# Two image layers on one core: the last band's filter taps held back until the third band of the next image, a reordered start of the query pass, and one band fewer on the array at the end

## The chip, the cores and the metric

The kernel runs on one core of a Trainium2 chip. The metric is the device time of one execution in microseconds (us). The profiler adds, for one execution, when each engine ran which instruction. The engines are named as in the profile: PE is TensorE (matmuls), PEld its weight loads, DVE VectorE, ACT ScalarE, POOL GpSimd, SP SyncE, which issues most of the DMAs.

## The reference

Eight images of 384 channels and 64 x 64 pixels pass through two layers, all in float32. Both add to their input.

```python
x = x + layer0(gn(x))     # gn: group norm over 32 groups
x = x + layer1(gn(x))

# layer 0: linear attention, 6 heads of 64
q = elu(rope(conv1x1(x, Wq)) * scale) + 1
k = elu(rope(conv1x1(x, Wk))) + 1
v = conv1x1(x, Wv)
kv, k_sum = sum_n k v, sum_n k
out = (q @ kv) / (q . k_sum + 1e-6);  conv1x1(out, Wfc)

# layer 1: a 1x1 convolution, a filter in the 8x8 Fourier domain, 3x3 taps, a gate
t = conv1x1(x, w_in);  t = irfft2(rfft2(blocks(t)) * fft_filter)
t = depthwise3x3(t, w_dw)
x1, x2 = t[:, :192], t[:, 192:]
return conv1x1(gelu(x1) * x2, w_out)
```

## The kernel before

An image is cut into eight bands of eight rows (512 pixels). A band is a tile of 128 partitions by three channel tiles by 512 pixels. The loop over images `b` has two passes over the bands of one image.

The first is `queries(b, ...)`: the end of layer 0. For each band, `q_project` makes three `pq` tiles (nine matmuls), the rotation and the elu turn them into `qc` on DVE and ACT (lines 610 to 626, then 337 to 339), `q_normalise` makes the normaliser with matmuls against `ks_bd` (`pn`, line 635) and a short chain of DVE and ACT steps that ends in `parts`, `q_spread` spreads that over the channels (`prb`, line 659) and multiplies `qc` by it (line 668), and `project_out` gives `pf` (line 676), which is added to `x`. Before the first band's output, `keys.finish` turns the accumulated keys and values into a matrix `mt` through `kx`, `ks_bd` and `pm`. Bands run two apart: `pq` of band j + 2, `pn` of band j + 1, `prb` of band j, `pf` of band j - 1.

The second pass is layer 1 of the image, mixed with the keys and values of image b + 1. Per band: `normalised` makes `hf`, `expand_filter` the matmuls `pi` and `pd` and the product `tf`, `back_transform` the matmuls `pb` and the ACT copies into one of two `ring` tiles with a halo row above and below. The last halo row of a band is filled from the band after it. Then `first_taps` (ACT, the first of nine taps), `taps` (24 DVE instructions, eight for each channel tile, line 788), `gate_taps` (gelu on ACT, product on DVE, into the single tile `gated`), and `contraction` (`pw`, lines 815 and 826, four ACT copies into `y`, and a DMA on POOL's queue that adds `y` to the output; line 845). `taps` run one band behind and `contract` two bands behind. The work that is left at the end of an image is done in the next image's `queries`: `before_last` contracts band 6, `gate` does taps and gate of band 7 after the first band's `q_spread`, and `output` contracts band 7 at the third band:

```python
            if j == 0:
                gate()
            ...
            if j == 2 and b < nb - 1:
                output()
            if j in (4, 5):
                load_x(b + 1, j - 4)
```

Between its layer 1 steps, a band of the second pass takes items from `fill`: `pk` and `pv` of a band and the accumulation of keys and values (line 470), 24 small matmuls of 1.6 us per band. Band 0 and band 1 accumulate themselves, band 2 nothing, and later bands the one before:

```python
                fill = chain_of(keys.project(j), keys.accumulate(j - 1 if j > 2 else NBAND))
```

The last image has no next image, so its second pass is a loop of its own. There, in the bands for which `on_array` is true (3, 6 and 7), the third channel tile's nine taps are matmuls with diagonal weights (`array_taps`, `ptap`, line 764), and DVE has 16 taps instead of 24.

The kernel gives the instructions in a written order, and a scheduler then orders each engine's queue by what can run when; for the order on an engine, the built order is shown where it matters. Tiles come from pools: nine `w` tiles, ten `x` tiles (which `y` shares), two `dw` tiles, and eight PSUM banks (`ps_tile`).

Of the kernel before, what the change touches and what calls it, by code (L numbers as in the profile page):

```python
# [9 lines left out]
F32 = mybir.dt.float32  # L10
BF16 = mybir.dt.bfloat16
AF = mybir.ActivationFunctionType
ALU = mybir.AluOpType

P = 128
C = 384
CT = 3
H = W = 64
N = H * W
NBAND = 8  # L20
# [97 lines left out]
def conv_blocks_kernel(ctx: ExitStack, tc: tile.TileContext, a: dict, out: bass.AP, nb: int):  # L118
    nc = tc.nc
# [9 lines left out]
    def ps_tile(name):  # L129
        return psum.tile([P, 512], F32, tag="ps", name=name)  # L130
# [9 lines left out]
    def load_x(b, j):  # L140
        if b >= nb:
            return
        t = xp.tile([P, CT, BT], F32, tag="x", name=f"x_{b}_{j}")
        nc.sync.dma_start(t, x_in[b][:, :, j * BT : (j + 1) * BT])
        xt[b, j] = t
# [96 lines left out]
    ident = groups[:, 2 * CT * NG :]  # L242
# [387 lines left out]
    def q_normalise(b, j, q):  # L630

        pn = ps_tile(f"pn_{b}_{j}")
        for t in range(CT):
            for s in range(4):
                nc.tensor.matmul(
                    pn[32 * s : 32 * s + 32, :P],
                    ks_bd[:, t, :],
                    q[:, t, s * P : (s + 1) * P],
                    start=(t == 0),
                    stop=(t == CT - 1),  # L640
                )
        rn = small.tile([P, P], F32, tag="rn", name=f"rn_{b}_{j}")
        nc.vector.tensor_scalar_add(rn, pn[:, :P], 1e-6)
        nc.vector.reciprocal(rn, rn)

        part = small.tile([P, P], BF16, tag="part", name=f"part_{b}_{j}")
        parts = small.tile([P, P], BF16, tag="parts", name=f"parts_{b}_{j}")
        nc.scalar.copy(part, rn)
        nc.vector.scalar_tensor_tensor(rn, part, take_off[:, 0:1], rn, ALU.mult, ALU.add)
        nc.scalar.copy(part, rn)  # L650
        nc.vector.scalar_tensor_tensor(parts, part, take_off[:, 1:2], rn, ALU.mult, ALU.add)
        return parts
# [19 lines left out]
    def project_out(b, j, q, mt):  # L672
        for m in range(CT):
            p_ = ps_tile(f"pf_{b}_{j}_{m}")
            for t in range(CT):
                nc.tensor.matmul(  # L676
                    p_, mt[:, t, m * P : (m + 1) * P], q[:, t, :], start=(t == 0), stop=(t == CT - 1)
                )
            xm = xt[b, j][:, m, :]
            nc.vector.scalar_tensor_tensor(xm, p_, bfc[:, m : m + 1], xm, ALU.add, ALU.add)  # L680
            if m == 0:
                yield
        if j == 1:
            differences[b] = taps_pool.tile([P, CT, BT], F32, tag="dw", name=f"differences_{b}")
        band_sums(b, 1, j, xt[b, j], differences.get(b))
# [64 lines left out]

    def on_array(b, j):

        return b == nb - 1 and j in (3, NBAND - 2, NBAND - 1)

    def make_diagonals():
        t = small.tile([P, CT, C], F32, tag="wk", name="diagonals", bufs=1).rearrange("p t c -> p (t c)")
# [21 lines left out]
            dw_pe[b, j] = ps_tile(f"ptap_{b}_{j}")  # L778
            array_taps(b, j, range(9 if j == NBAND - 1 else 6))

    def taps(b, j):

        t, acc = ring[j % 2], dw[b, j]
        for m in range(CT - on_array(b, j)):
            for k in range(1, 9):
                src = t[:, m, k // 3 : k // 3 + 8, k % 3 : k % 3 + W]
                wd = w_dw[:, m, k : k + 1]
                nc.vector.scalar_tensor_tensor(acc[:, m], src, wd, acc[:, m], ALU.mult, ALU.add)  # L788

    def gate_taps(b, j):  # L790
        g = gated
# [9 lines left out]
    def depthwise_gate(b, j):  # L801
        taps(b, j)
        gate_taps(b, j)
# [43 lines left out]
    def contract(b, j):  # L847
        run(contraction(b, j))
# [14 lines left out]
    def chain_of(*chains):  # L863
        for c in chains:
            yield from c

    def run(*chains):

        chains = list(chains)
        while chains:  # L870
            chains = [c for c in chains if next(c, chains) is not chains]
# [62 lines left out]
                    sum_weight(self.wv, "wv")  # L934
                self.vbias = v_bias(self.b, self.params)

    def queries(b, keys, before_last, gate, output):


        wq, qbias = keys.wq, keys.qbias  # L940
        q, done = {}, []
        run(q_project(b, 0, wq, qbias, q))
        before_last()
        run(keys.accumulate(NBAND - 1))
        finish = keys.finish(done)
        for _ in zip(q_project(b, 1, wq, qbias, q), finish):
            pass
        prepared = []
        chain = layer0_chain(b + 1, prepared)
        normaliser = {0: q_normalise(b, 0, q[0])}  # L950
        for j in range(NBAND):

            if j < NBAND - 2:
                project = q_project(b, j + 2, wq, qbias, q)
                for _ in range(2 if j else CT):
                    next(project)
                if j == 0:
                    run(finish)
                    mt = done[0]
                if j != 1:  # L960
                    normaliser[j + 1] = q_normalise(b, j + 1, q[j + 1])
                run(project)
            if 2 <= j < NBAND - 2:
                next(chain, None)
            q_spread(b, j, q[j], normaliser.pop(j))
            if j == 0:
                gate()
            if j >= 1:
                output_ = project_out(b, j - 1, q.pop(j - 1), mt)
                if j in (1, NBAND - 2):  # L970
                    next(output_)
                    normaliser[j + 1] = q_normalise(b, j + 1, q[j + 1])
                run(output_)
                if j < NBAND - 2:
                    next(chain, None)
            if j == 2 and b < nb - 1:
                output()
            if j in (4, 5):
                load_x(b + 1, j - 4)
            if j == NBAND - 2:  # L980
                run(chain)
        run(project_out(b, NBAND - 1, q.pop(NBAND - 1), mt))
        return prepared

# [6 lines left out]
    prepared = []  # L991
# [51 lines left out]
    def nothing():  # L1043
        pass

    before_last = gate = output = nothing
    for b in range(nb):
        prepared = queries(b, keys, before_last, gate, output)
        keys = Keys(b + 1, prepared)
        params = []  # L1050
        chain, more = norm_chain(b, 1, params), chain_of(keys.project_k(0), keys.load_values(), keys.project_k(1))
        last = b == nb - 1
        if last:

            more = contraction(b - 1, NBAND - 1) if b else iter(())
        for steps in (2, 0, 1, 1) if last else (2, 1, 1, 3):
            next(chain)
            for _ in range(steps):
                next(more, None)
        run(chain)  # L1060
        ahead = normalised(b, 0, params, (8, 8), "f")
        run(more)
        if last:
            break
        first_values = keys.project_v(0)
        next(first_values, None)
        for j in range(NBAND):
            if j < 2:
                fill = chain_of(keys.project_v(j) if j else first_values, keys.accumulate(j))
            else:  # L1070
                fill = chain_of(keys.project(j), keys.accumulate(j - 1 if j > 2 else NBAND))
            tf = []
            h = normalised(b, j, params, (8, 8), "f") if j else ahead
            store_x(b, j)
            if 1 <= j < NBAND - 1:
                load_x(b + 1, j + 1)
            layer1 = expand_filter(b, j, h, tf)
            items = 1 if j < 2 else 2

            def some(n):  # L1080
                for _ in range(n):
                    next(fill)

            next(layer1)
            some(items)
            run(layer1)
            some(2 * items)
            back_transform(b, j, tf[0])
            first_taps(b, j)
            some(items)  # L1090
            if j > 1:
                contract(b, j - 2)
            run(fill)
            keys.prepare(j)
            if j > 0:
                depthwise_gate(b, j - 1)
            stream_stats(b + 2, j)
        keys.prepare(NBAND)

        def before_last(b=b):  # L1100
            contract(b, NBAND - 2)

        def gate(b=b):
            depthwise_gate(b, NBAND - 1)

        def output(b=b):
            contract(b, NBAND - 1)


    make_diagonals()  # L1110
# [2 lines left out]
    for j in range(NBAND):  # L1113
        tf = []
        layer1 = expand_filter(b, j, h, tf)
        run(layer1)
        store_x(b, j)
        if j < NBAND - 1:
            h = normalised(b, j + 1, params, (8, 8), "f")
        back_transform(b, j, tf[0])  # L1120
        if j and on_array(b, j - 1):

            array_taps(b, j - 1, range(6, 9))
        first_taps(b, j)
        if j >= 2:
            contract(b, j - 2)
        if j >= 1:
            taps(b, j - 1)
            gate_taps(b, j - 1)
# [45 lines left out]
```

## Time and profile before

| | |
|---|---|
| median of three executions | 3442.15 us (3442.06 to 3443.75) |
| profiled execution | 3442.33 us, span 3440.6 us |
| mean granted TensorE clock | 0.989 |
| PE busy | 96% of the span |
| DVE busy | 81% |
| ACT busy | 57% |
| POOL busy | 4% |
| DMA | 336.01 MB, mean 98 GB/s |

The span runs from the first to the last instruction of the profiled execution; 1.7 us lie around it. In a row for a stretch of time stand its bounds and length, then the busy time of PE, PEld, DVE, ACT and POOL, each with its number of instructions, the granted clock, the DMA share and the rate. In a row of a timeline stand the start, the time taken, the engine, the line of the kernel, the operation, output and inputs, and in brackets the idle time before it and what ended it. A float32 matmul leaves two records. The second image's first pass begins at about 570 us and its layer 1 at about 750; each later image lies some 420 us further on, and the last pass runs from about 3240 us to the end.

### The profile page before, as it was taken

The numbers are of one execution on the slowest core, as the hardware profiler recorded it, in microseconds if no ns is written. First come the engines' busy times: TensorE is split into PE (matmuls) and PEld (weight loads), VectorE is DVE, ScalarE is ACT, GpSimd is POOL, SyncE is SP. The second block draws the span as 40 slices with busy tenths as digits, with TensorE's granted clock in tenths as the row PEclk, the third lists the DMA queues.
The fourth block names the chain that finished last, engine by engine and source line by source line (L and its number), as shares of the span: only waits on it lengthen the run. The fifth ranks groups of instructions, "written<-read, shape, count | busy, mean of one in ns | idle before, by whom it ended". The sixth has DMA issues, their size and how long they took to land.

```text
span 3440.6 us, 53200 instructions
## 1 busy us (share of the span) xinstructions
PE 3319.7 (96%) x21374; PEld 1856.2 (54%) x21374; DVE 2786.9 (81%) x4430; ACT 1976.0 (57%) x3854; POOL 143.2 (4%) x247
## 2 busy tenths in 40 slices
PE   8999999999999999999999999989999899999987
PEld 5544565456654566445664456644566445664454
DVE  6587789868898688986889868897788977899597
ACT  4445666556664566555665556655576555555553
POOL 0000001000010000100001000010000000000000
PEclk9999999999999999999999999999999999999999
DMA  6323244332343333442343423334243331333112
GB/s 221 112 89 115 65 111 100 114 124 66 92 112 115 110 84 87 100 131 96 82 108 90 133 90 92 94 98 131 81 111 92 107 121 55 66 83 101 51 27 48
DMA packets 149484, 336.01 MB, mean 98 GB/s; under 512 B 27141, under 2 KB 38389, under 8 KB 141045
## 3 DMA queue, kind: packets, MB, share of 16 engines
q1 hardware_dynamic: 123844, 282.85, 24.5%
q0 software_dynamic: 25200, 49.55, 10.0%
q8 instruction: 168, 2.75, 0.3%
q14 instruction: 80, 0.65, 0.1%
q10 hardware_dynamic: 192, 0.21, 0.0%
HBM read 232.70 MB, written 99.88 MB: 97 GB/s over the span
## 4 chain that ended last, share of the span: by engine, by line
PE 76%; DVE 18%; ACT 4%; issue 1%; DMA 0%; SPq 0%; DVEq 0%; ACTq 0%
PE pi L694 14%; PE pk L438 13%; PE pf L676 13%; PE pv L454 12%; PE pq L597 7%; DVE dw L788 6%; PE pw L815 4%; PE pd L708 2%; PE pb L729 2%; PE pw L826 2%; PE acc L483 2%; PE acc L470 2%; DVE qc L339 1%; DVE qc L610 1%; ACT ring L739 1%
## 5 line engine op out<-in xcount | busy, mean ns | idle before, releaser
L788 DVE SCALAR_TENSOR_TENSOR dw<-ring,w_dw,dw 128x512 f32<-128x512 f32 x1512 | 1059.5, 749 | 262.5 <-ACT ring L745 223.9
L438 PE MATMUL pk<-wk,x 128*128 128x384 f32 x1536 | 545.0, 496 | 0.0
L676 PE MATMUL pf<-qc,mt 128*128 128x512 f32 x1152 | 518.8, 604 | 17.1 <-DVE qs L610 17.0
L597 PE MATMUL pq<-x,wq 128*128 128x512 f32 x1152 | 528.1, 607 | 0.1
L694 PE MATMUL pi<-w_in,hf 128*128 128x384 f32 x1536 | 516.1, 492 | 1.3 <-ACT hf L332 1.3
L454 PE MATMUL pv<-wv,x 128*128 128x384 f32 x1344 | 470.0, 488 | 0.0
L438 PEld LDWEIGHTS pk<-wk,x 128*128 128x128 f32 x1536 | 283.5, 191 | 205.3 <-issue 32.5
L694 PEld LDWEIGHTS pi<-w_in,hf 128*128 128x128 f32 x1536 | 287.8, 191 | 196.3 <-issue 4.6
L676 PEld LDWEIGHTS pf<-qc,mt 128*128 128x128 f32 x1152 | 214.8, 191 | 271.3 <-issue 231.8
L597 PEld LDWEIGHTS pq<-x,wq 128*128 128x128 f32 x1152 | 215.2, 193 | 255.8 <-issue 244.4
L454 PEld LDWEIGHTS pv<-wv,x 128*128 128x128 f32 x1344 | 253.6, 190 | 181.4 <-issue 8.4
L461 ACT COPY v<-pv 128x384 f32<-128x384 f32 x224 | 108.8, 486 | 417.8 <-PE pv L454 417.1
L680 DVE SCALAR_TENSOR_TENSOR x<-pf,bfc,x 128x512 f32<-128x512 f32 x192 | 141.1, 744 | 103.9 <-PE pf L676 103.2
L624 ACT ACTIVATE qs<-pq,qbias 64x512 f32<-64x512 f32 x128 | 87.6, 685 | 193.4 <-DVE qc L610 175.1
L701 ACT COPY ht<-pi 128x384 f32<-128x384 f32 x256 | 114.9, 484 | 114.7 <-PE pi L694 111.6
L815 PE MATMUL pw<-gated,w_out 128*128 128x256 f32 x768 | 177.5, 380 | 0.2 <-DVE gated L795 0.2
L441 DVE TENSOR_TENSOR kc<-pk,kbias 128x384 f32<-128x384 f32 x256 | 141.1, 551 | 40.9 <-PE pk L438 40.9
L337 ACT ACTIVATE qs<-qc 128x1536 f32<-128x1536 f32 x64 | 95.1, 1486 | 135.9 <-DVE qc L626 125.8
L845 POOL DMA_DIRECT2D out_dram<-y x63 | 80.7, 1281 | 2068.8 <-DVE dw L788 1047.8
L179 ACT ACTIVATE differences<-x,shift 128x512 f32<-128x512 f32 x168 | 120.2, 716 | 76.6 <-DVE x L680 76.6
L815 PEld LDWEIGHTS pw<-gated,w_out 128*128 128x128 f32 x768 | 145.0, 190 | 34.7 <-issue 5.7
L337 ACT ACTIVATE ks<-kc 128x1536 f32<-128x1536 f32 x64 | 95.2, 1487 | 100.9 <-DVE kc L445 72.0
(171 smaller groups left out, 4384.4 us busy)
## 6 DMA issues: line engine op xcount, KB each, us to landing
tq<-in_tq SPq DMA_DIRECT2D x64, 1024.0 KB, 4.8
x<-in_x SPq DMA_DIRECT2D x64, 768.0 KB, 5.9
tk<-in_tk SPq DMA_DIRECT2D x64, 768.0 KB, 4.4
out_dram<-x SPq DMA_DIRECT2D x63, 768.0 KB, 3.3
out_dram<-y POOLq DMA_DIRECT2D x63, 768.0 KB, 7.8
xs<-in_x SPq DMA_DIRECT2D x56, 768.0 KB, 5.9
wk<-in_wk SPq DMA_DIRECT2D x8, 576.0 KB, 3.8
wfc<-in_wfc SPq DMA_DIRECT2D x8, 576.0 KB, 7.7
```

What stands on the lines that cost most here:

```text
L179: nc.scalar.activation(out[:, m, :], x_[:, m, :], AF.Identity, bias=shift[:, m : m + 1], accum_out=of_m[0])
L337: nc.scalar.activation(e, x_, AF.Relu, scale=-1.0)
L438: nc.tensor.matmul(pk[:, :C], tokens(t), wks[:, t, :], start=(t == 0), stop=(t == CT - 1))
L441: nc.vector.tensor_add(kc[:, i, :], pk[:, :C], bias)
L454: nc.tensor.matmul(pv[:, :C], xt[b, j][:, t, i * P : (i + 1) * P], wvs[:, t, :], start=(t == 0), stop=(t == CT - 1),)
L597: nc.tensor.matmul(p_, wqs[:, t, m * P : (m + 1) * P], xt[b, j][:, t, :], start=(t == 0), stop=(t == CT - 1),)
L676: nc.tensor.matmul(p_, mt[:, t, m * P : (m + 1) * P], q[:, t, :], start=(t == 0), stop=(t == CT - 1))
L680: nc.vector.scalar_tensor_tensor(xm, p_, bfc[:, m : m + 1], xm, ALU.add, ALU.add)
L694: nc.tensor.matmul(p_[:, :C], h[:, t, i * P : (i + 1) * P], w_in[:, t, :], start=(t == 0), stop=(t == CT - 1),)
L701: nc.scalar.copy(ht[:, i, :], p_[:, :C])
L788: nc.vector.scalar_tensor_tensor(acc[:, m], src, wd, acc[:, m], ALU.mult, ALU.add)
L815: nc.tensor.matmul(p_[h][:, m - m0, :], w_out[:, 0, m * P : (m + 1) * P], gated[:, h * HT : (h + 1) * HT], start=(m == m0), stop=False,)
```

## The change

It has four parts.

`last_band(b)` is a generator that takes the place of `gate` and `output`. It is stepped once in each band from the third on. Its first step does the eight taps of channel tile 0, then a matmul of the identity with `w_dw` and a DVE copy of the result, `late_w`. The next steps do the taps of tiles 1 and 2 with `late_w` in place of `w_dw`, then the gate, then the contraction. The built order puts that matmul on PE behind `pf` of band 1, and puts the contraction behind `pf` of band 4.

`queries` is written out anew. `q_spread` of band 0 comes ahead of `pq` of band 3; `pn` of band 1 comes after the first `pq` tile of band 3, and `prb` of band 1 after the first `pf` tile. The steps of the next image's normalisation (`chain`) come one band later, and the loads of the next image's first two bands stand in bands 5 and 6.

In the second pass, bands 0 and 1 are accumulated one band later each.

In the last image, band 3 is no longer on the array, and the last three `array_taps` of band 6 are issued from `taps`, after `pw` of band 5.

```diff
     def on_array(b, j):
 
-        return b == nb - 1 and j in (3, NBAND - 2, NBAND - 1)
+        return b == nb - 1 and j >= NBAND - 2
...
+    def tile_taps(b, j, m, weights):
+
+        t, acc = ring[j % 2], dw[b, j]
+        for k in range(1, 9):
+            src = t[:, m, k // 3 : k // 3 + 8, k % 3 : k % 3 + W]
+            wd = weights[:, m, k : k + 1]
+            nc.vector.scalar_tensor_tensor(acc[:, m], src, wd, acc[:, m], ALU.mult, ALU.add)
+
     def taps(b, j):
-
-        t, acc = ring[j % 2], dw[b, j]
+        if on_array(b, j) and j < NBAND - 1:
+            array_taps(b, j, range(6, 9))
         for m in range(CT - on_array(b, j)):
...
+            tile_taps(b, j, m, w_dw)
...
-    def queries(b, keys, before_last, gate, output):
+    def queries(b, keys, before_last, late):
...
-        normaliser = {0: q_normalise(b, 0, q[0])}
-        for j in range(NBAND):
-
+
+        normalise(0)
+        run(q_project(b, 2, wq, qbias, q))
+        run(finish)
+        mt = done[0]
+        q_spread(b, 0, q[0], normaliser.pop(0))
+        project = q_project(b, 3, wq, qbias, q)
+        next(project)
+        normalise(1)
+        run(project)
+        output_ = project_out(b, 0, q.pop(0), mt)
+        next(output_)
+        q_spread(b, 1, q[1], normaliser.pop(1))
+        normalise(2)
+        run(output_)
+        for j in range(2, NBAND):
             if j < NBAND - 2:
                 project = q_project(b, j + 2, wq, qbias, q)
...
+                normalise(j + 1)
                 run(project)
...
-            if j == 0:
-                gate()
...
-            if j == 2 and b < nb - 1:
-                output()
-            if j in (4, 5):
-                load_x(b + 1, j - 4)
             if j == NBAND - 2:
-                run(chain)
+                next(output_)
+                normalise(j + 1)
+            run(output_)
+            if j < NBAND - 2:
+                next(chain, None)
+            if j == 5:
+                load_x(b + 1, 0)
+            next(late, None)
+            if j == 6:
+                load_x(b + 1, 1)
+        run(chain)
...
+    def last_band(b):
+
+        tile_taps(b, NBAND - 1, 0, w_dw)
+
+        ps = ps_tile(f"pwd_{b}")
+        nc.tensor.matmul(
+            ps[:, : CT * 9], ident, w_dw.rearrange("p t k -> p (t k)"), start=True, stop=True
+        )
+        late_w = small.tile([P, CT, 9], F32, tag="late_w", name=f"late_w_{b}", bufs=1)
+        nc.vector.tensor_copy(late_w, ps[:, : CT * 9].rearrange("p (t k) -> p t k", t=CT))
+        yield
+        for m in range(1, CT):
+            tile_taps(b, NBAND - 1, m, late_w)
+            if m == CT - 1:
+                gate_taps(b, NBAND - 1)
+            yield
+        if b + 1 < nb - 1:
+            contract(b, NBAND - 1)
...
             if j < 2:
-                fill = chain_of(keys.project_v(j) if j else first_values, keys.accumulate(j))
+                fill = chain_of(keys.project_v(j) if j else first_values, keys.accumulate(j - 1))
             else:
-                fill = chain_of(keys.project(j), keys.accumulate(j - 1 if j > 2 else NBAND))
+                fill = chain_of(keys.project(j), keys.accumulate(j - 1))
...
-        def gate(b=b):
-            depthwise_gate(b, NBAND - 1)
-
-        def output(b=b):
-            contract(b, NBAND - 1)
+        late = last_band(b)
...
         back_transform(b, j, tf[0])
-        if j and on_array(b, j - 1):
-
-            array_taps(b, j - 1, range(6, 9))
         first_taps(b, j)
```

More of the change, by code (lines that the diff above doesn't have):

```diff
@@ L779, in first_taps @@
             array_taps(b, j, range(9 if j == NBAND - 1 else 6))
+    def tile_taps(b, j, m, weights):
[4 more added lines that the diff above has]
+            nc.vector.scalar_tensor_tensor(acc[:, m], src, wd, acc[:, m], ALU.mult, ALU.add)
     def taps(b, j):
-        t, acc = ring[j % 2], dw[b, j]
+        if on_array(b, j) and j < NBAND - 1:
+            array_taps(b, j, range(6, 9))
         for m in range(CT - on_array(b, j)):
[L785 to L788, printed above, removed]
+            tile_taps(b, j, m, w_dw)
     def gate_taps(b, j):
@@ L935, in prepare, with normalise @@
                 self.vbias = v_bias(self.b, self.params)
-    def queries(b, keys, before_last, gate, output):
+    def queries(b, keys, before_last, late):
         wq, qbias = keys.wq, keys.qbias
-        q, done = {}, []
+        q, done, normaliser = {}, [], {}
+        def normalise(j):
+            normaliser[j] = q_normalise(b, j, q[j])
         run(q_project(b, 0, wq, qbias, q))
@@ L949, in queries @@
         chain = layer0_chain(b + 1, prepared)
-        normaliser = {0: q_normalise(b, 0, q[0])}
-        for j in range(NBAND):
+        normalise(0)
[13 more added lines that the diff above has]
+        for j in range(2, NBAND):
             if j < NBAND - 2:
                 project = q_project(b, j + 2, wq, qbias, q)
-                for _ in range(2 if j else CT):
+                for _ in range(2):
                     next(project)
-                if j == 0:
[L958 to L961, printed above, removed]
+                normalise(j + 1)
                 run(project)
-            if 2 <= j < NBAND - 2:
                 next(chain, None)
             q_spread(b, j, q[j], normaliser.pop(j))
-            if j == 0:
-                gate()
[L968 to L975, printed above, removed]
-            if j == 2 and b < nb - 1:
-                output()
-            if j in (4, 5):
-                load_x(b + 1, j - 4)
-            if j == NBAND - 2:
-                run(chain)
+            output_ = project_out(b, j - 1, q.pop(j - 1), mt)
+            if j == NBAND - 2:
+                next(output_)
[9 more added lines that the diff above has]
+        run(chain)
         run(project_out(b, NBAND - 1, q.pop(NBAND - 1), mt))
@@ L1044, in nothing @@
         pass
-    before_last = gate = output = nothing
+    def last_band(b):
[14 more added lines that the diff above has]
+            contract(b, NBAND - 1)
+    before_last, late = nothing, iter(())
     for b in range(nb):
-        prepared = queries(b, keys, before_last, gate, output)
+        prepared = queries(b, keys, before_last, late)
         keys = Keys(b + 1, prepared)
@@ L1081, in some @@
                 for _ in range(n):
-                    next(fill)
+                    next(fill, None)
             next(layer1)
```

## The prediction

> **What bounds the kernel now.** I read the page's busy shares, then busy time by stretch, the waits in total, and the timelines of the places found. An image takes some 420 us, so one boundary between images stands for all.
>
> ```profile
> PE 3319.7 (96%) x21374; PEld 1856.2 (54%) x21374; DVE 2786.9 (81%) x4430; ACT 1976.0 (57%) x3854; POOL 143.2 (4%) x247
> ```
>
> ```profile
> 560.00:600.00 40.00, 38.20 (x229) 21.01 (x229) 39.77 (x59) 23.48 (x35) 8.62 (x14) 1.00 0.55 134
> 600.00:640.00 40.00, 32.10 (x176) 14.29 (x174) 39.50 (x70) 19.47 (x26) 0.00 (x0) 0.96 0.21 73
> 640.00:680.00 40.00, 39.74 (x174) 19.56 (x174) 30.56 (x58) 21.65 (x42) 1.41 (x2) 1.00 0.54 154
> 680.00:720.00 40.00, 40.00 (x182) 17.54 (x182) 32.14 (x52) 23.27 (x51) 0.14 (x1) 1.00 0.33 111
> ```
>
> TensorE is busy 96%, so only its 121 us of idle time and its slowed stretches can be won. The stretch rows (PE busy is the second number, DVE's the fourth) show the boundary of the second image: from 560 to 640 VectorE is full and TensorE starves for 1.8 + 7.9 us; from 640 to 720 TensorE is full and VectorE has 17 us free. The kernel is TensorE-bound except at seven such boundaries and in the last pass from 3240.
>
> ```profile
> PE pn L635 <- DVE qc L339: 36.1, 20, 3.4
> PE pf L676 <- DVE qs L610: 17.0, 12, 1.8
> ...
> PE acc L470 <- ACT v L461: 6.9, 6, 1.1
> ```
>
> The waits (us in total, times, longest) name the boundary's two, 53 us, and a third with another cause: the second band's accumulation waits for the ACT copy of its values, six times 1.1 us.
>
> ```profile
> 605.73 0.86 PE L635 MATMUL pn<-qc,ks_bd 128*32 128x128 f32 x24 [3.13 <-DVE qc L339]
> 606.52 0.35 PE L659 MATMUL prb<-parts,expand 32*128 32x128 bf16 x12
> 606.80 9.69 PE L597 MATMUL pq<-x,wq 128*128 128x512 f32 x18
> ...
> 622.84 5.42 PE L676 MATMUL pf<-qc,mt 128*128 128x512 f32 x12 [1.78 <-DVE qs L610]
> ```
>
> TensorE's timeline there: each wait is for a VectorE step of the query chain, queued behind filter taps. Nine `pq` matmuls (18 records) take 9.69 us after the longest wait, elsewhere 7.99: a slowed clock, another 1.7 us per boundary.
>
> ```profile
> 3309.13 1.49 DVE L716 TENSOR_TENSOR tf<-pd,filt 128x384 f32<-128x384 f32 x3
> ...
> 3336.38 1.95 DVE L716 TENSOR_TENSOR tf<-pd,filt 128x384 f32<-128x384 f32 x4 [0.26 <-PE pd L708]
> ...
> 3315.64 7.81 PE L764 MATMUL ptap<-ring,diagonals 128*128 128x512 f32 x12 [1.91 <-ACT ring L744]
> ```
>
> The last pass: from one band's `tf` to the next takes 27.25 us where TensorE computes band 3's taps (`ptap`), ahead of `pw` and the next `pi`; the band before took 19.7.
>
> **What the skill says.** The Trainium skill, "TensorE: Matmul & The Clock Gate", section "What's actually happening": an idle window of about 3.4 us brings the array to half clock, and about as long a busy one releases it. The trace agrees in kind: the slow `pq` follows 3.13 us of waiting, and the slice's clock is 0.96. The same page, "Architectural detail", says that VectorE and ScalarE are strict FIFO; so a tap queued ahead of a query step delays it, as above. "PSUM — Partial Sum Buffer", "Specifications (TRN2)", gives eight banks: a matmul can wait for a bank still being read. "ScalarE: Activation LUTs", "What ACT_TABLE_LOAD costs", gives 1283 ns per load; the trace has 1283.
>
> **The change, part by part** (second image; its times before).
>
> *Late taps.* `last_band` takes 16 of the last band's 24 taps out of 570-624 and makes them wait for `late_w`, whose matmul stands behind `pf` of band 1. A tap takes 0.66 us of VectorE (nine in 6.05): 10.6 us, and the three gate multiplications (0.69 + 0.42 + 0.42) go along: 12.1 us leave the full stretch. Channel tile 0's eight taps are held by nothing and stay. Walking the built order with these durations: kernel-map copies and `qc` of band 0 end about 0.5 to 1.6 us earlier; `pn` of band 0 then waits for GpSimd's `ks_bd` copies (585.72 to 592.26), so 1.3 us of TensorE idle remain there. `pn` of band 1 now stands behind the first `pq` tile of band 3 and is covered. The second `pq` tile of band 3 takes the PSUM bank of band 0's first `prb`, and waits for its multiplication, behind the `mt` copies and a 1.66 us addition: about 2 us. I find no further wait up to `pf` of band 1, which ends at 648.25 before. So 9.97 us of idle (1.80 + 7.90 + 0.26) become 3.3: **6.7 us** on each of six boundaries, 40 us. The seventh has 8.5 us (page stretches 3080 to 3200): **5 us**. With no wait of 3 us left, the slow clock goes: 1.7 x 7 = **12 us**.
>
> *Where they go.* From band 2 on VectorE takes 12.1 us more and 0.2 for the copy, against 17 free to 720 and 7 more to 731. Queued behind the new wait for `late_w` are one tap, then `qc` of band 4; its matmul is one small record group, so under 0.5 us. Following bands 2 to 5, VectorE stays 1 to 3 us ahead of TensorE's needs, so I charge nothing; without that cover each us late costs 7 us in all. The added identity matmul: 0.3 us by the 0.35 of the `ps_m` rows, 7 times, **-2 us**. ACT moves three gelus with their table loads (as many loads in the built order) into 640 to 720, where it has 35 us free.
>
> *The output of the last band* (12 matmuls in 24 records, 4 ACT copies, one accumulating DMA) moves from band 2 behind `pf` of band 4: the same 4.3 us of TensorE. SP moves `x(b+1,0)` ahead of four `tq` loads; it waits for an earlier `y`, which left at 568.7, so `tq` isn't held. `x(b+1,1)` moves behind `wq`, `tk` and a store, and waits for the band's own output DMA: `pw` ends near 696, copies 2, issue 1.3, landing 7.7, load 5.9: about 713, needed near 731 by `pk`: 18 us to spare. Queued behind it on SP are stores and `wv`, not needed before `pv` at 750. Free. The small `ps_m`, `ps_mc`, `ps_v`, `ps_r` of the next normalisation come one band later, still well ahead of `wk`: free.
>
> *Accumulation one band later.* Bands 0 and 1 are accumulated in bands 1 and 2: same matmuls (1.6 us each), and the ACT copy is then a band old. **6.9 us**. What was the cover behind `pb` of band 0 is gone; the next `pi` needs `hf` of band 1, done at 764.2, and starts at 768.5: no wait.
>
> *The end.* Band 3 leaves TensorE: 9 matmuls (18 records, 10.5 us) go, VectorE gets 8 taps (5.3 us), ACT one first tap. An off-array band is VectorE's own sum: 24 x 0.66 + 1.5 + 1.9 = 19.3; measured 19.7. Bands 3 to 5 took 27.25 + 21.2 + 18.7 = 67.2 (`tf` starts at 3309.13, 3336.38, 3357.59, 3376.33) and become 3 x 19.7 = 59.1: **8 us**. Bands 6 and 7 stay on the array; the last three of band 6's taps now stand behind `pw` of band 5, and walking the rest gives the old 38 us from `tf` of band 7 to the end, within 1.
>
> Sum: 40 + 5 + 12 + 7 + 8 - 2 = 70 us. The profiled execution took 3442.33 (span 3440.6 and 1.7 around it), the median is 3442.15, 0.2 below: **3372 us**.
>
> **Bounds of what isn't seen.** The boundary after: at best no idle (10 + 1.7 us each), at worst latency keeps half of it and the slow clock. Bands 2 to 5: a gain is excluded, since TensorE is already full there; a loss up to the 3 us by which my lead estimates may err, 21 us. The end: from 0 (TensorE's waits set the pace after all) to 10.
>
> **The rivals.**
> - *The chain, not the load, holds TensorE.* Each query step passes VectorE, ACT and back; `pn` still waits, and bands 2 to 5 give something back. For it: my own walk leaves two waits, and ACT is only half busy. Against it: VectorE is at 99% with taps between the steps. Half of the idle stays, no clock comes back: 7 x 3.5 + 7 + 8 - 2 = 37 us, 3405.
> - *Everything closes.* GpSimd and the PSUM bank are met as well: 68 + 12 + 7 + 8 - 2 = 93 us, 3349.
> - *The end doesn't shorten.* VectorE is 98% busy from 3280 to 3320, and the 5.3 us of taps lie on its path: 70 - 8 - 5 = 57, 3385. Against it: the 27 us band shows VectorE waiting too.
> - *Slower: `x(b+1,1)` comes late.* Its load hangs on the last band's output DMA, near 706. If that DMA and the queue ahead of it took 18 us longer, `pk` would stop; from another 10 us on (70 over 7 boundaries) the kernel is slower; 40 us late gives 3442 - 70 + 7 x 22 = 3526. Landings of 7.8 us (median) in the page speak against it.
> - *The taps don't move.* Excluded: they wait for `late_w` in the built order.
>
> **How the numbers follow.** Main case 0.62; chain 0.20; everything closes 0.10; end not shorter 0.05; late load 0.03. A measurement of this kernel can tell about 0.2% from no change, 7 us; all cases but the last lie beyond it on the fast side, and I leave 0.02 for a mixture that comes out even: faster 0.95, same 0.02, slower 0.03. The range reaches to the first and second rivals, 3349 to 3403: it leaves out the far half of the chain case and the late load.
>
> **What would show it.** Right: in the profile after, PE idle from 560 to 680 near 3 us with the clock at 1.00; `pn <- qc` down from 36.1 to under 10; `acc <- v` gone; VectorE near 38 of 40 in the 80 us after; `tf` to `tf` near 20 us in bands 3 to 5. Wrong: a new row of PE waiting for `qc` or `parts` in bands 2 to 5; PE `pk` waiting for a DMA; the end's bands over 22 us.

## Result and profile after

The changed kernel takes 3393.27 us (median of four, 3391.38 to 3402.41) against 3442.43: ratio 0.9862, 95% interval 0.9844 to 0.9880. That is 49 us faster, where 70 were forecast. The profiled executions took 3442.33 and 3393.96 us, with spans 48.4 us apart.

The engine row of the page after:

```profile
PE 3302.1 (97%) x21370; PEld 1851.0 (55%) x21370; DVE 2787.5 (82%) x4445; ACT 1975.6 (58%) x3855; POOL 130.5 (4%) x247
```

The span less TensorE's busy time was 120.9 us of idle; it is now 90.1. So 30.8 of the 48.4 us are idle time, and 17.6 are time in which TensorE counted as busy, 11.8 of them `ptap` of the band that left the array (28.1 to 16.3 us).

The boundary of the second image by stretch (PE is the second number, DVE the fourth, the granted clock the seventh):

```profile
560.00:600.00 40.00, 38.74 (x241) 20.89 (x239) 37.31 (x60) 25.43 (x35) 6.64 (x14) 1.00 0.58 144
600.00:640.00 40.00, 36.64 (x179) 16.57 (x180) 38.08 (x64) 17.66 (x26) 0.00 (x0) 1.00 0.27 96
640.00:680.00 40.00, 40.00 (x173) 18.12 (x172) 37.55 (x69) 23.63 (x49) 0.14 (x1) 1.00 0.29 105
680.00:720.00 40.00, 37.10 (x174) 17.54 (x174) 27.66 (x47) 22.25 (x49) 1.43 (x2) 0.96 0.44 114
```

From 560 to 640 VectorE now has 4.6 us free where it had 0.7, and TensorE starves for 1.26 + 3.36 us from 560 to 680 instead of 9.97. But the last row is new: from 680 to 720, where TensorE was full before, it idles 2.9 us, and the clock falls to 0.96 there. What it waits for, over the whole kernel (us in total, times, longest):

```profile
PE pf L676 <- DVE qc L668: 17.4, 6, 2.9
PE pq L597 <- DVE qc L339: 16.4, 7, 2.3
PE pb L729 <- DVE tf L716: 14.2, 7, 3.6
PE pq L597 <- DVE qc L668: 7.1, 4, 1.8
...
PE pn L635 <- DVE qc L339: 1.4, 1, 1.4
```

`pn <- qc` fell from 36.1 to 1.4, and the accumulation's wait for `v` is gone. The first row did not exist before: `pf` of band 5, once in each of six images, waits for the multiplication of band 6's `qc` by `prb`. TensorE's timeline of the second image shows the three places:

```profile
601.58 2.84 PE L597 MATMUL pq<-x,wq 128*128 128x512 f32 x6 [2.35 <-DVE qc L339]
...
606.99 5.42 PE L597 MATMUL pq<-x,wq 128*128 128x512 f32 x12 [1.78 <-DVE qc L668]
...
699.87 4.54 PE L676 MATMUL pf<-qc,mt 128*128 128x512 f32 x6 [2.90 <-DVE qc L668]
```

The first two are `pq` of band 3, in the old boundary. For the first of them the profile names the addition of line 339, which ended at 601.56; ScalarE's copies of band 2's third `pq` tile (line 624) ended at 601.52, and the weight loads of the waiting matmuls name these, at seven places with 17.6 us:

```profile
PEld pq L597 <- ACT qs L624: 17.6, 7, 2.5
```

At the third place, the waiting group takes 4.54 us; the same three matmuls take 2.84 at 601.58. That is the slowed clock, 1.7 us, at a new place.

Why is that multiplication late? VectorE's timeline ahead of it:

```profile
692.86 2.06 DVE L680 SCALAR_TENSOR_TENSOR x<-pf,bfc,x 128x512 f32<-128x512 f32 x3
694.84 1.07 DVE L352 TENSOR_SCALAR wq<-wq,rs 128x384 f32<-128x384 f32 x3
697.59 1.76 DVE L339 SCALAR_TENSOR_TENSOR qc<-qc,qs 128x1536 f32<-128x1536 f32 x1 [1.69 <-ACT qs L338]
699.27 1.94 DVE L668 TENSOR_TENSOR qc<-qc,prb 128x384 f32<-128x384 f32 x4
```

VectorE itself stands idle for 1.69 us: the last step of band 7's `qc` (line 339) waits for ScalarE's exponential, and band 6's multiplications are queued behind it. ScalarE's timeline:

```profile
685.23 1.28 ACT L803 ACT_TABLE_LOAD   x1
686.53 0.42 ACT L803 ACTIVATE gelu<-dw 64x256 f32<-64x256 f32 x1
686.85 0.40 ACT L803 ACTIVATE gated<-dw 64x256 f32<-64x256 f32 x1
...
694.78 1.28 ACT L338 ACT_TABLE_LOAD   x1
696.08 1.48 ACT L338 ACTIVATE qs<-qs 128x1536 f32<-128x1536 f32 x1
```

The late band's gelus load their table between the exponentials of bands 6 and 7, and the exponential has to load its own again. This reading is a theory until a kernel without the loads has run.

The end, by `tf` (bands 3 to 7):

```profile
3272.39 1.49 DVE L716 TENSOR_TENSOR tf<-pd,filt 128x384 f32<-128x384 f32 x3
...
3292.29 1.95 DVE L716 TENSOR_TENSOR tf<-pd,filt 128x384 f32<-128x384 f32 x4
...
3311.97 1.49 DVE L716 TENSOR_TENSOR tf<-pd,filt 128x384 f32<-128x384 f32 x3
...
3331.74 1.95 DVE L716 TENSOR_TENSOR tf<-pd,filt 128x384 f32<-128x384 f32 x4
3355.61 1.95 DVE L716 TENSOR_TENSOR tf<-pd,filt 128x384 f32<-128x384 f32 x4
```

The intervals are 19.9, 19.7 and 19.8 us where they were 27.25, 21.21 and 18.74; the last is 23.9, before 25.9.

### The profile page after: what moved, and what is told of

Same layout as the page of the kernel before. It is cut to its first block, busy times and chain, and to the rows that moved or that the text cites. A ratio compares the mean times of both kernels' runs of the same rounds, so it can differ in the third digit from the quotient of the medians.

```text
span 3392.2 us, 53266 instructions
## 1 busy us (share of the span) xinstructions
PE 3302.1 (97%) x21370; PEld 1851.0 (55%) x21370; DVE 2787.5 (82%) x4445; ACT 1975.6 (58%) x3855; POOL 130.5 (4%) x247
## 3 DMA queue, kind: packets, MB, share of 16 engines
q1 hardware_dynamic: 123844, 282.85, 24.9%
## 4 chain that ended last, share of the span: by engine, by line
PE 77%; DVE 16%; ACT 4%; issue 2%; DMA 1%; SPq 0%; DVEq 0%; ACTq 0%
PE pi L694 13%; PE pf L676 13%; PE pk L438 13%; PE pv L454 13%; PE pq L597 8%; DVE dw L787 6%; PE pw L820 3%; PE pb L729 3%; PE pd L708 2%; PE acc L470 2%; PE acc L483 2%; PE pw L831 2%; DVE qc L626 1%; DVE qc L610 1%; DVE qc L339 1%
## 5 line engine op out<-in xcount | busy, mean ns | idle before, releaser
L787 DVE SCALAR_TENSOR_TENSOR dw<-ring,w_dw,dw 128x512 f32<-128x512 f32 x1408 | 983.9, 749 | 243.7 <-ACT ring L745 205.1
L676 PE MATMUL pf<-qc,mt 128*128 128x512 f32 x1152 | 517.6, 602 | 17.4 <-DVE qc L668 17.4
```

Source lines behind the costliest of these rows:

```text
L676: nc.tensor.matmul(p_, mt[:, t, m * P : (m + 1) * P], q[:, t, :], start=(t == 0), stop=(t == CT - 1))
```

## Experiments

The kernel before took 3442 to 3443 us beside each group of runs. The changed kernel ran again beside three of them:

> The changed kernel itself, unaltered, so that the three that follow stand beside it on one chip. 3393 as at first; if chip and day move it, up to 3400, since its three parts alone added to 42 us and not to 49.

Measured: 3398.39 us, ratio 0.9872 (0.9859 to 0.9886), with the same wait rows. Its single times lie between 3392.43 and 3403.69, a wider spread than before's; the last section returns to that.

### The three parts alone

On the kernel before, with the accumulation alone moved:

```diff
-fill = chain_of(keys.project_v(j) if j else first_values, keys.accumulate(j))
+fill = chain_of(keys.project_v(j) if j else first_values, keys.accumulate(j - 1))
...
-fill = chain_of(keys.project(j), keys.accumulate(j - 1 if j > 2 else NBAND))
+fill = chain_of(keys.project(j), keys.accumulate(j - 1))
```

> The kernel before with one part of the change alone: every band's kernel map accumulates one band later. Both theories: the six waits of acc for v (6.9 us) go and nothing takes their place, so about 3435.5 us (7 us faster). If a wait of pb for tf or of pi for hf takes their place, 3440 to 3443.

Measured: 3433.71, ratio 0.9973 (0.9962 to 0.9984), 9.4 us. The row of `acc` waiting for `v` is gone and none takes its place.

With the new end alone (`on_array` for bands 6 and 7, band 6's last three array taps inside `taps`):

> The kernel before with the new end alone: band 3 of the last pass leaves TensorE, band 6's last taps stand behind pw of band 5. By the sum on record 8 us, 3434. By the profile of the changed kernel, where tf of band 3 to the end takes 119.8 us instead of 131.5, 11.7 us: 3430.7. If so, the term of the end was too small, and the 21 us that are missing are all at the boundaries, with 3.7 more.

Measured: 3430.06, ratio 0.9965 (0.9952 to 0.9979), 13.0 us. The larger of the two figures is the nearer one, though the interval (7 to 17 us) holds both.

The changed kernel without these two parts:

> The changed kernel without the later accumulation and without the new end: the new query pass and the late taps alone. Theory A (all that is missing is lost inside the query pass, in the new wait of pf of band 5 and the slow clock after it): 3393.3 + 6.9 + 11.7 = about 3412, 30 us faster than before, and the row of pf waiting for qc stays at 17.4 us. Theory B (the three parts get in each other's way, so that the loss is in none of them alone): near 3442 - 57 = 3385 to 3390, and the pf row gone.

Measured: 3423.65, ratio 0.9943 (0.9930 to 0.9955): 19.5 us faster than before. Its profile has the same new wait:

```profile
PE pf L676 <- DVE qc L668: 17.3, 6, 2.9
PE pq L597 <- DVE qc L339: 16.3, 7, 2.3
```

So theory A holds as to place, not as to its figure of 30 us (the interval is 15 to 24): the query pass was to bring 55 us and brings some 20, or 21 to 27 if the other two parts, as measured, are taken off the whole, while these two bring what they should or more. The three alone add to 42 us; the whole brings 44 to 49. With intervals of some 4 us or more to either side, no interaction is shown.

### Which cause: the bank or the chain

In the changed kernel's built order, `pf` of band 5 takes the PSUM bank of band 6's first `prb`. One more step puts `pw` a band later, and `pf` then takes a bank that was long free:

```diff
             yield
+        yield
         if b + 1 < nb - 1:
             contract(b, NBAND - 1)
```

> The changed kernel with the output matmuls of the last band (pw) one band later, behind pf of band 5. In the built order pf of band 5 then takes a PSUM bank that was read long before, not that of band 6's first prb. Theory A1 (the bank is what counts): the row of pf waiting for qc, 17.4 us, goes with nothing in its place, some 20 us faster than the changed kernel, about 3373. Theory A2 (band 7's query chain is late on VectorE and ScalarE, whichever bank is taken): pn of band 7, next in TensorE's order, waits for the same addition qc of band 7, which ended at 699.3 in the second image; TensorE has 4.3 us less to do before it, so the wait is 4 us or more instead of 2.9, no faster than the changed kernel: 3393 to 3405. The load of x(b+1,1) comes a band later as well: if pk then waits for it, slower still.

Measured: 3407.49, ratio 0.9898 (0.9885 to 0.9912). The `pf` row is gone, and `pn` of band 7 waits instead:

```profile
PE pn L635 <- DVE qc L339: 22.8, 7, 3.6
```

3.56 us in the second image, until 699.43, the time at which the other version's wait ended (699.87) but for the step in between. A2 holds: band 7's chain is late, and TensorE meets it at whichever instruction comes first. The bank only decided which. `pw` had been cover. The wait is a little shorter than the 4 us expected and the time above the expected range: TensorE idles 95.4 us, 5 more than in the changed kernel, and is busy 12 us longer with the same instructions.

### What makes the chain late

The three gelus of the late band became plain copies, so that this version leaves a part of the computation out:

```diff
-                gate_taps(b, NBAND - 1)
+                gate_taps(b, NBAND - 1, AF.Copy)
```

> The changed kernel with the three gelus of the late band made plain copies (its gelu is left out at seven bands): the same ScalarE instructions without their table loads, two of 1.28 us between the exponentials of bands 0 and 1 and two in band 7's chain. Theory L (the loads make band 7's chain late): the wait of pf of band 5 falls from 2.9 us to between 0.3 and 1.6, its row from 17.4 to 2 to 10, and the wait of pq of band 3 by about 1.3 us. Theory V (VectorE's queue makes it late: taps, gate products and three output additions ahead of the addition qc of band 7): the row stays within 2 us of 17.4. Time against the changed kernel, 3398: 3370 to 3385 in L, 3393 to 3400 in V; slow clock moves either by 10.

Measured: 3375.42, ratio 0.9804 (0.9790 to 0.9817), 18 to 23 us less than the changed kernel (3393.27 and 3398.39). Its waits:

```profile
PE prb L659 <- DVE parts L651: 13.6, 7, 2.0
PE pf L676 <- DVE qc L668: 9.0, 6, 1.5
```

The `pf` wait fell by 1.4 us, near the 1.28 of one table load; of the two in that stretch, only the exponential's was on the chain, since in the changed kernel ScalarE waited another 0.57 us for VectorE after the gelus. The other 1.5 us are not the loads'. VectorE's timeline of this version shows them:

```profile
695.31 1.76 DVE L339 SCALAR_TENSOR_TENSOR qc<-qc,qs 128x1536 f32<-128x1536 f32 x1 [0.72 <-ACT qs L338]
...
696.99 1.94 DVE L668 TENSOR_TENSOR qc<-qc,prb 128x384 f32<-128x384 f32 x4
```

`prb` of band 6 ended at 696.09, but its multiplications started at 696.99, again behind the addition of band 7: 0.9 us. The first of them takes the other 0.6, up to `pf` at 697.59. At the boundary the 2.35 us wait of `pq` went, and `prb` of band 1, next in line, waits 1.95. So theory L is shown for about half of the `pf` wait. The rest is read from VectorE's queue in this one timeline; no run takes it away by itself.

### Where the late work could go

The gate and tile 2 a band earlier:

```diff
-            if m == CT - 1:
-                gate_taps(b, NBAND - 1)
-            yield
+        gate_taps(b, NBAND - 1)
+        yield
```

> The changed kernel with channel tile 2's taps and the gate made in the same step as tile 1's, a band earlier, and so pw behind pf of band 3. Its gelus then come ahead of band 6's exponential, which loads its table in any case; band 7's has no load ahead of it, no gate products and no taps. Theory A2 (band 7's chain is late because of the late band's work in it): the wait of pf of band 5 (17.4 us) goes, with the slow clock after it where there is one (about 1.7 us at two or three of six boundaries), and some 17 to 25 us come back against the changed kernel: 3368 to 3376. Rival: the same work makes band 6's chain late instead, and pn of band 6 or prb of band 5 waits some 3 us: no gain.

Measured: 3440.11, ratio 0.9993 (0.9985 to 1.0001), 42 us more than the changed kernel beside it. The rival came true, and more: 16 taps and the gate now stand in one band.

```profile
PE pn L635 <- DVE qc L339: 28.9, 7, 6.1
PE pf L676 <- DVE qs L610: 18.0, 7, 2.9
```

The first row had 1.4 us in the changed kernel, the second is new; the `pf` row of 17.4 us is gone, as theory A2 said. TensorE idles 111.1 us, 21 more than in the changed kernel, and is busy 25 us longer with the same instructions: the clock. Together they eat the whole gain, though six table loads were saved (72 for the exponential instead of 78).

Tile 0's last tap held by the copied weights, so that its gelu leaves the boundary:

```diff
-        tile_taps(b, NBAND - 1, 0, w_dw)
+        tile_taps(b, NBAND - 1, 0, w_dw, range(1, 8))
...
+        tile_taps(b, NBAND - 1, 0, late_w, [8])
```

> The changed kernel with the last of channel tile 0's eight late taps reading the copied weights as well, nothing else. Its gelu, which stood between the exponentials of bands 0 and 1 and cost two table loads of 1.28 us there, then comes behind band 4's. Theory C (at the boundary ScalarE's chain now holds TensorE: pq of band 3 waits 2.34 us for the ScalarE copy of band 2's third tile, queued behind the second load): the wait falls by 1.3 us or more at 7 boundaries, and the slow clock after it goes at the 5 to 7 boundaries where there is one: 9 + 8 to 12 = 17 to 21 us against the changed kernel. Rival: VectorE's queue holds it as much (the copies of mt and the addition of band 2): 0 to 5 us. The wait of pf of band 5 stays in both.

Measured: 3403.82, ratio 0.9884 (0.9869 to 0.9900), not faster than the changed kernel. The `pq` wait did go, but `prb` of band 1 waits 1.95 us:

```profile
PE pf L676 <- DVE qc L668: 17.3, 6, 2.9
PE prb L659 <- DVE parts L651: 13.6, 7, 2.0
```

In the profiled execution, the slowest of four, TensorE idles 84 us in all, 6 less than in the changed kernel, and is busy 20 us longer (3322.5 against 3302.1) with the same instructions: the clock. Neither the theory's sum nor the rival's had that.

Both edits together:

> Both edits together. If A2 and C hold, their gains add: 35 to 45 us against the changed kernel, 3350 to 3360. If VectorE is what is full in bands 2 to 5, one of the waits comes back elsewhere and the sum is under 25.

Measured: 3431.65, ratio 0.9970 (0.9958 to 0.9981), 33 us more than the changed kernel: not even part of the sum. The rows of the full band are there again (`pf` 22.6 us, `pn` 17.5).

All 24 taps held:

```diff
-        tile_taps(b, NBAND - 1, 0, w_dw)
...
+        tile_taps(b, NBAND - 1, 0, late_w)
```

> The changed kernel with all 24 taps of the late band held by the copied weights, not 16. The boundary loses 8 more taps (5.3 us of VectorE) and the two table loads; bands 2 to 5 get both. In the built order pf of band 5 no longer stands behind the addition qc of band 7: two of band 6's four multiplications come ahead of it. If the boundary is bound by VectorE's queue and ScalarE's loads, both its waits go (23 us) and the pf row as well, less about 1 us for pn of band 7: 3360 to 3380. Rival (bands 2 to 5 are full, as the version with the gate a band earlier showed): pn of bands 6 or 7 waits 3 to 6 us at each boundary, 3400 to 3440.

Measured: 3411.25, ratio 0.9908 (0.9894 to 0.9921). Both `pq` rows are gone and the `pf` row fell to 5.5 us, as the built order said, but three rows grew:

```profile
PE pf L676 <- DVE qs L610: 19.0, 13, 2.6
PE pt L583 <- DVE kvt_bd L571: 17.5, 12, 2.5
...
PE pn L635 <- DVE qc L339: 9.2, 8, 2.6
```

The first stands in bands 2 to 5 (2.59 us at 669.43 in the second image; the version with the gate a band earlier waits 2.87 us at 670.25). That is the rival, though it named `pn`, which waits 2.6 us at most and not 3 to 6. The middle row is at the boundary itself: with no taps between, band 0's `qc` is done sooner, and in ScalarE's queue its exponential (with a table load) gets ahead of the copy of `kx` for which `kvt_bd` waits.

### Is the hold needed?

The late taps read the ordinary weights, so nothing holds them but their place in the program:

```diff
-            tile_taps(b, NBAND - 1, m, late_w)
+            tile_taps(b, NBAND - 1, m, w_dw)
```

> The changed kernel with its late taps reading the weights that the other bands read, so that only their place in the program is late and nothing holds them (the matmul and copy of weights stay, unread). Theory H (the hold is what empties the boundary): in the built order 12 of the 24 taps or more then run before the first pf additions, the waits of band 1's chain come back by 4 to 6 us in some 7 boundaries, and the wait of pf of band 5 goes with the work that left bands 4 and 5: 3400 to 3425. Rival (the order of the query pass alone does it, the hold costs more than it gives): 3375 to 3395, faster than the changed kernel.

Measured: 3387.36, ratio 0.9836 (0.9822 to 0.9849), 11 us less than the changed kernel's 3398.39 (0.9859 to 0.9886) and 6 less than its first 3393.27. The slowest of its five executions took 3388.40, the fastest of the changed kernel's eight 3391.38. The rival holds, not theory H. Its waits:

```profile
PE pq L597 <- ACT qs L624: 16.9, 7, 2.5
...
PE pq L597 <- DVE qc L668: 7.7, 7, 2.0
...
PE pn L635 <- DVE qc L339: 6.7, 7, 1.0
```

Fifteen taps instead of eight run at the boundary (nine are left after it), and its waits come to 31.3 us instead of 24.9: 6.4 us lost in all, not 4 to 6 per boundary. The `pf` row of 17.4 is absent. The exponential's loads show one reason (ScalarE's groups of the changed kernel, then of this one):

```profile
L338 ACT ACT_TABLE_LOAD x78 | 100.1, 1283 | 1.4
```

```profile
L338 ACT ACT_TABLE_LOAD x72 | 92.4, 1283 | 1.3
```

Six fewer, one for each boundary at which a next image is normalised. Free to run earlier, the two gelus now follow the square root of the next image's normalisation, after which the exponential must load its table anyway, and band 7's chain has none. The seven taps that went forward have left VectorE's queue in bands 4 and 5 as well (the last late tap ends at 668.84, in the changed kernel at 685.54), and `pf` of band 5 no longer starts behind a multiplication. How much each of these gave was not separated.

Last, without the hold and without the copied weights, the taps cut so that tile 0's gelu falls behind band 4's exponential:

```diff
+        tile_taps(b, NBAND - 1, 0, w_dw, range(1, 8))
+        yield
+        tile_taps(b, NBAND - 1, 1, w_dw, range(1, 5))
+        tile_taps(b, NBAND - 1, 2, w_dw, range(1, 8))
+        yield
+        tile_taps(b, NBAND - 1, 0, w_dw, range(8, 9))
+        tile_taps(b, NBAND - 1, 2, w_dw, range(8, 9))
+        tile_taps(b, NBAND - 1, 1, w_dw, range(5, 9))
+        gate_taps(b, NBAND - 1)
+        yield
```

> No hold, no copied weights and no matmul for them; the late taps are cut so that the gelu of tile 0 becomes ready behind band 4's exponential and the other two between the square root of the next image's normalisation and band 6's exponential (both by the built order): no gelu between bands 0 and 1, none in band 7's chain, and one table load more than in the version without the hold. Theory L, carried over from the version without gelus: pq of band 3 no longer waits 2.4 us, prb of band 1 waits 2.0 instead, pf of band 5 doesn't wait; against the version without the hold (3387) some 8 to 10 us by the waits and 2 for the matmul: 3372 to 3380. Rival: the two loads and the gelu ahead of band 5's exponential (3.2 us) make pn of band 5 or prb of band 4 wait 1 to 3 us at seven boundaries: 3388 to 3405.

Measured: 3383.36, ratio 0.9829 (0.9815 to 0.9842), the fastest version with the full computation, though its interval overlaps the one before it. The time lies between the theory's 3380 and the rival's 3388. The text expected one table load more than there; the profile has the same number. The `pq` waits shrank from 24.6 us to 6.5 and `prb` waits 11.7 as foreseen. A row that was not foreseen takes some back:

```profile
PE ps_r L281 <- DVE rsg L310: 11.0, 14, 2.4
```

It had 4.6 us in the changed kernel and 5.0 in the version before this one. Probably the next image's normalisation (`rsg`) now meets VectorE at a worse time; no run here shows it.

## Why the prediction was right, and where 21 us went

The time fell inside the range, and at the boundary itself the mechanism was the one named: `pn <- qc` fell from 36.1 us to 1.4. What was given back in bands 2 to 5 was not in the sum. That the time still fell inside is in part luck: 3.7 us at the end and some 6 us that no term names made up for part of it, and the slowest of the changed kernel's eight executions, 3403.69, lies just outside. The terms, forecast and found in the profiled executions:

| term | forecast | found |
|---|---|---|
| idle, six boundaries (58.2 before, 40.0 after) | 40 | 18.2 |
| idle, the seventh (3080 to 3262 before, 12.4; 3048 to 3225 after, 9.6) | 5 | 2.8 |
| accumulation (idle between boundaries, 6.9 to 1.2) | 6.9 | 5.7 |
| end (first `tf` to the end, 178.6 to 166.9) | 8 | 11.7 |
| copying matmuls | -2 | -2.7 |
| slowed clock (found: what the other rows leave over) | 12 | 12.7 |
| sum | 70 | 48.4 |

**Idle at the boundary: the step that failed.** Under "Where they go" the forecast charged nothing for bands 2 to 5, because VectorE would stay 1 to 3 us ahead. The new wait of `pf`, 6 x 2.9 = 17.4 us, stands there; without it the six boundaries would have brought 35.6 of the 40. The text priced this case, at 7 us for each us late and 21 at worst, and named its sign, TensorE waiting for `qc` in bands 2 to 5. What it missed, for about half of the wait, was not VectorE's load but a chain through ScalarE: it counted the moved gelus' loads ("as many loads in the built order") against ScalarE's 35 free us, and not by where they stand. One of them stood in band 7's chain, and the run without gelus shows it to be about half of the wait. Behind late work the question is not whether an engine has time to spare but whether the next query step is queued behind it. The lead on VectorE was wrong too: without the loads band 6's multiplications still started 0.9 us after `prb`.

The remaining 4.4 us are of two kinds. Six boundaries were reckoned at 9.97 us of idle, 59.8, and had 58.2. And 22.6 us stayed in them besides the `pf` wait, not 19.8. In the second image `pn` of band 0, forecast to wait 1.3 us for GpSimd, doesn't wait, and instead the first `pq` tile of band 3 waits 2.35 for another cause, ScalarE's copy of band 2's third tile. The second tile, forecast at 2 us, waits 1.78. In three of the six images the first tile runs at the slowed clock (4.54 us instead of 2.84) and the second wait is gone. The seventh boundary's 5 us were reckoned on 3080 to 3200, where 8.5 us of idle became 4.2; behind that stretch idle grew by 1.4.

**The slow clock did not go.** "With no wait of 3 us left, the slow clock goes" is refuted. Adding (1 - granted clock) x 20 us over stretches of 20 us from 40 to 3140 gives 15.8 us before, 10.2 after and 10.6 in the repeat: 5 to 6 us came back, not 12. The 10.2 are six groups, each some 1.7 us longer: three of `pf` behind the new wait and three of the first `pq` tile of band 3. The latter cost nothing: the slowed tile takes the place of the second wait, and the next tile starts 5.41 us after it, slowed (1016.88 to 1022.29) or not (601.58 to 606.99). The rest of that row of the table is 1.4 us of idle in the first image (1.15 of it the sixth wait of the accumulation) and some 6 us of TensorE's busy time that I can't assign; the ends of matmuls are modelled, and the accumulation, 9.4 us when run alone, may hold part of it.

**The end** was mis-sized low. Bands 3 to 5 became 59.35 us where 59.1 was forecast. Bands 6 and 7, set at no change "within 1", shortened by 2.0 and 1.8 us.

**The accumulation** was right: its row is gone, with all of its 6.9 us. The load of `x(b+1,1)`, forecast free, was: no row of `pk` waiting for a DMA appears, not even in the version with `pw` a band later.

**The rivals.** "The chain, not the load, holds TensorE" (3405) had much of the mechanism, bands 2 to 5 giving something back: 21 us of the boundaries' idle came back, under a third, and part of the clock, of which it had nothing. The better end, that part of the clock and the unassigned busy time kept the time below its figure. "The end doesn't shorten" and the late load were wrong, "everything closes" far off.

## To carry to other kernels

When work moves from a full stretch into a slack one, follow each chain that passes there from engine to engine; here a table load between two exponentials delayed the chain by about its own length (1.4 us for 1.28), with ScalarE busy only 58% of the time. A wait removed at one matmul came back at the one next in order, so cover is better read from the built order than from free microseconds. And try the move without its hold: here the scheduler, left free, found a place for the gelus that cost a load less, and the hold lost 6 to 11 us.

## Unexpected in the hardware

The lowered clock does not follow from the length of a wait alone. The Trainium skill, "TensorE: Matmul & The Clock Gate", section "What's actually happening", puts it after an idle window of about 3.4 us and calls that window free-running. Here, in the version without gelus, three of seven waits of 1.95 us were followed by it: at two of these, twelve records of `pf` took 7.11 us instead of 5.42.

```profile
1024.61 0.35 PE L659 MATMUL prb<-parts,expand 32*128 32x128 bf16 x12 [1.95 <-DVE parts L651]
...
1025.68 5.42 PE L676 MATMUL pf<-qc,mt 128*128 128x512 f32 x12
...
1847.44 0.35 PE L659 MATMUL prb<-parts,expand 32*128 32x128 bf16 x12 [1.95 <-DVE parts L651]
...
1848.51 7.11 PE L676 MATMUL pf<-qc,mt 128*128 128x512 f32 x12
```

After the 2.34 us wait of `pq`, the group was slow in three of seven places in the changed kernel and in four in its repeat: the same three, and the second image besides (fast at 601.58, slow at 602.15). After the 2.9 us wait of `pf` it was slow in three of six places and in two of the repeat's, and in all six of the version with tile 0's tap held, where it took 5.49 us instead of 2.84. What decides it stays open: the place of a wait in such a window could matter, but a wait of 1.95 us can't fill one, and no run here tests it. The changed kernel's times scatter over 11 us with it: the mean granted clock was 0.990 to 0.992 in the five executions below 3395 us and 0.988 to 0.989 in the three above 3401. It is also why a version with 6 us less idle was no faster.

The same skill's "ScalarE: Activation LUTs", section "What ACT_TABLE_LOAD costs", adds a drain of about 1.38 us to each load. No run here shows it: the load at 694.78 follows the instruction before it at once and the exponential starts 0.02 us after its end, and taking the load away shortened the wait by 1.4 us, not 2.7.
